# A causal convolution as diagonal matmuls, spaced pieces in the first scan, and fresh slot budgets

## The chip, the cores and the metric

The kernel runs on one core of a Trainium2 chip. A core has TensorE (PE in the profile; its weight loads are listed as PEld), VectorE (DVE), ScalarE (ACT), GpSimd (POOL), and the queue of SyncE (SP) that issues most DMAs. Each engine works through its own queue in order and waits for semaphores of the others. The metric is the device time of one launch in microseconds; of several runs the median counts.

## The reference, cut to what matters

The input is x of 4 batches, 256 positions and 256 features. A layer with a selective scan comes first, and then a layer with 16 attention heads and a mixture of 16 experts of which each token uses 4. All is float32.

```python
xz = einsum('bld,ed->ble', x, W_in); xp, z = split(xz, 2)          # 512 channels each
xpad = pad(xp, 3 positions ahead)
xc = silu(conv_b + sum(xpad[:, k:k + l, :] * conv_w[:, k] for k in range(4)))
dbc = einsum('ble,fe->blf', xc, W_x)                               # dt (128), Bm (16), Cm (16)
delta = softplus(einsum('blr,er->ble', dt, W_dt) + b_dt)
dA = exp(delta[..., None] * A); dBx = delta[..., None] * Bm * xc[..., None]
h = dA_t * h + dBx_t                                               # step by step, 16 states a channel
y = (einsum('bles,bls->ble', hs, Cm) + xc * Dp) * silu(z)
x = layernorm(x + einsum('ble,de->bld', y, W_out))
...
x = layernorm(x + ffn(x))                                          # attention, then the experts
```

The change bears on the sum over the four taps k for one of the four batches, and on the order of work around it.

## The kernel before

**Layout.** Channels lie on the 128 partitions. The 512 channels are four groups of 128, taken as two pairs p (0 and 1), so that a tile of 128x512 holds two groups of 256 positions. A *unit* is one of the 16 states n for one pair p, named n_p: 32 units make the scan of a batch, and 128 that of the four batches, in one stream.

**A unit.** decay (L463, ScalarE, two exponentials) writes da, of which there is one tile for each pair. feed (L472, GpSimd) writes dbx (three buffers). scan (L480, VectorE) writes h, a single buffer in PSUM. weigh (L487) multiplies by C into hc (two buffers), on VectorE, or for some units of the first batch (1_0, 2_1, 4_0 and so on) on GpSimd, where h lies in the hc tile itself. add is a pair of matmul pieces into y_ps for the first batch (L494, TensorE), and an addition on GpSimd (L492) for the others.

**The front of a batch.** conv_steps(b) projects a pair (project, L243, four matmuls, into one of the PSUM banks that bank() hands out in turn); last_tap (L259, ScalarE) multiplies by the last tap and adds the bias; tap (L251, VectorE) adds the other three taps for each of the two groups, six instructions a pair; tanh (L347, ScalarE) and one multiplication (L349, VectorE) make xc. delta_steps(b) projects xc to dbc (L362), copies B and C out (bc_sb, L367) and sends them through DRAM, from where they come back spread over all partitions (bc, L455, two loads for four units, two buffers), and begins delta (L377, L380, L383). soft_steps(b) ends the softplus: exp (L394), w (L398, L400), a logarithm (L407, with two loads of activation tables), additions on GpSimd and VectorE (L410, L413), and u = delta * xc (L415). z_steps(b) makes the gate.

**Two phases.** The first batch's front (first_front) is written out by hand. Then the first loop (N_RAMP = 34 units) runs the first batch's scan, and weaves in the front of the second batch, conv_steps(1), delta_steps(1), soft_steps(1). weave(engines) is called twice for each unit; in each call every row of jobs may give out its next piece, if that piece's engine is among those named; after a piece of TensorE, a piece of ScalarE or VectorE must let `lag` calls pass. Here lag is 2 and budgets do not hold pieces back (free=True), but their costs are taken off the budgets all the same.

Then come the slots (L1271), one for each of the 64 attention heads and three to end. A slot holds fixed pieces of three heads (projection of q and k at L591, scores, softmax, values, output at L672), three units of the scan in the first six slots and two after, and calls of weave, which hold a piece back while its engine's budget is below zero. At the start of each slot a budget gains a share (2816 for TensorE, 2000 for ScalarE and VectorE), up to that share. conv_steps(2), delta_steps(2), soft_steps(2) and z_steps(1) are jobs of the first 16 slots. After the last slot the remaining experts and the final norm follow.

SyncE's queue also carries 64 fills of a table in DRAM with zeros (L200), most of them during the first scan.

Of the kernel before, what the change touches and what calls it, by code (L numbers as in the profile page):

```python
# [10 lines left out]
F32 = mybir.dt.float32  # L11
I32 = mybir.dt.int32
AF = mybir.ActivationFunctionType
ALU = mybir.AluOpType
# [4 lines left out]
P = 128  # L19
B, S, D = 4, 256, 256  # L20
# [5 lines left out]
NC = DI // P  # L26
NS = 16
DC = 4
NH = 16
HG = 4  # L30
HD = 128
# [22 lines left out]
def block_kernel(  # L54
# [18 lines left out]
    nc = tc.nc  # L73
    TB = S // P
    NP = NC // 2
# [13 lines left out]

    chan_sb = const.tile([P, NC, DC + 3 + NS], F32, name="chan_sb")  # L90
    conv_w = lambda c, k: chan_sb[:, c, k : k + 1]
    conv_b = lambda c: chan_sb[:, c, DC : DC + 1]
    b_dt = lambda c: chan_sb[:, c, DC + 1 : DC + 2]
    d_skip = lambda c: chan_sb[:, c, DC + 2 : DC + 3]
    a_neg = const.tile([P, NC, NS], F32, name="a_neg")
    norms_sb = const.tile([P, 2, KD], F32, name="norms_sb")
    gate_sb = const.tile([P, KD, NE], F32, name="gate_sb")
    ident = const.tile([P, P], F32, name="ident")
# [10 lines left out]
    sh_down = const.tile([P, NSC, D], F32, name="sh_down")  # L109
    w_o_sb = const.tile([P, NH, D], F32, name="w_o_sb")  # L110

# [24 lines left out]
    m_w = mamba.enter_context(tc.tile_pool(name="m_w", bufs=1))  # L136
    m_x = mamba.enter_context(tc.tile_pool(name="m_x", bufs=2))
    m_keep = mamba.enter_context(tc.tile_pool(name="m_keep", bufs=1))
    m_two = mamba.enter_context(tc.tile_pool(name="m_two", bufs=2))
    m_tmp = mamba.enter_context(tc.tile_pool(name="m_tmp", bufs=4))  # L140
# [5 lines left out]
    w_x_sb = m_w.tile([P, NC, P + 2 * NS], F32, name="w_x_sb")  # L146
    w_dt_sb = m_w.tile([P, NC, P], F32, name="w_dt_sb")
    w_out_sb = m_w.tile([P, NC, D], F32, name="w_out_sb")

    xts = {}  # L150

# [17 lines left out]

    nc.vector.tensor_scalar_mul(chan_sb[:, :, 0 : DC + 1], chan_sb[:, :, 0 : DC + 1], 0.5)  # L170
    nc.scalar.activation(a_neg, chan_sb[:, :, DC + 3 :], AF.Exp)
    nc.vector.tensor_scalar_mul(a_neg, a_neg, -1.0)
# [35 lines left out]
    def bank(shape, name):  # L208
        banks.append(banks.pop(0))
        return banks[-1][0].tile(shape, F32, tag=banks[-1][1], name=name)  # L210
# [18 lines left out]
    OP, TINY = 60, 120  # L229
    PE, ACT, DVE, POOL, LATER = "PE", "ACT", "DVE", "POOL", "LATER"  # L230


    xcs, zss, deltas, us, ys, bcs = {}, {}, {}, {}, {}, {}

    def pair(pool, tag, b):
        return [pool.tile([P, 2, S], F32, tag=f"{tag}{p}", name=f"{tag}{b}_{p}") for p in range(NP)]

    def project(b, m, pt=None):
        if pt is None:
            pt = bank([P, 2, S], f"xz{b}_{m}")  # L240
        for j in range(2):
            for k in range(KD):
                nc.tensor.matmul(  # L243
                    pt[:, j, :], w_in_sb[:, m + j, k, :], xts[b][:, k, :], start=(k == 0), stop=(k == KD - 1)
                )
        return pt

    def tap(acc, pt, p, j):
        for k in range(DC - 1):
            o = DC - 1 - k  # L250
            nc.vector.scalar_tensor_tensor(  # L251
                acc[:, j, o:], pt[:, j, 0 : S - o], conv_w(2 * p + j, k), acc[:, j, o:], ALU.mult, ALU.add
            )

    def last_tap(b, p, pt):
        acc = m_tmp.tile([P, 2, S], F32, tag="t", name=f"acc{b}_{p}")
        for j in range(2):
            c = 2 * p + j
            nc.scalar.activation(acc[:, j, :], pt[:, j, :], AF.Identity, bias=conv_b(c), scale=conv_w(c, DC - 1))  # L259
        return acc  # L260

    def first_front():
# [70 lines left out]
        next_x(0)  # L333
        return y_ps

    def conv_steps(b):
        xc = xcs[b] = pair(m_two, "xc", b)
        for p in range(NP):
            yield PE, 4 * S
            pt = project(b, 2 * p)  # L340
            yield ACT, 2 * S
            acc = last_tap(b, p, pt)
            for j in range(2):
                yield DVE, 3 * (S + OP)
                tap(acc, pt, p, j)
            yield ACT, 2 * S
            nc.scalar.activation(pt, acc, AF.Tanh)  # L347
            yield DVE, 2 * S + OP
            nc.vector.scalar_tensor_tensor(xc[p], pt, 1.0, acc, ALU.add, ALU.mult)  # L349
# [201 lines left out]
    def load_v(b, g):  # L551
        wvs[b, g] = v_in.tile([P, KD * HG * HD], F32, tag="wv", name=f"wv{b}_{g}")
        nc.sync.dma_start(wvs[b, g], w_qkv[g][:, 2, :])

    class Values:
# [16 lines left out]
        def keep(self):  # L572
            b, g, i = self.b, self.g, self.i
            nc.scalar.copy(vs[b, g][:, i, :], self.pt)
            if i == TB - 1 and b * NH + (g + 1) * HG < B * NH:
                load_v(b + (g + 1) // (NH // HG), (g + 1) % (NH // HG))

# [79 lines left out]

    heads = [Head(b, hd) for b in range(B) for hd in range(NH)]


    def out_steps(b, slot):

        for hd in range(NH):
            while slot() < b * NH + hd + 3:
                yield LATER, 0
# [494 lines left out]

    budget = {PE: 0, ACT: 0, DVE: 0}

    def weave(*engines, lag=1, free=False):

        for name, row in work.items():
            while row:
                job = at_work.get(name) or next((j for j in row if j.may_begin(row)), None)
                if job is None:
                    break
                at_work[name] = job  # L1170
                if job.next is None or job.next[0] == LATER:
                    job.next = next(job.steps, ())
                if job.next:
                    engine, cost = job.next
                    job.since += 1
                    if engine not in engines or engine in (ACT, DVE) and job.since <= job.lag:
                        break
                    if not free and not job.urgent and budget.get(engine, 0) < 0:
                        break
                    if engine in budget:  # L1180
                        budget[engine] -= cost
                    job.next = next(job.steps, ())
                    job.lag, job.since = (lag if engine == PE else 0), 0
                if job.next:
                    if engine == DVE and job.next[0] == DVE:
                        continue
                    break
                row.remove(job)
                del at_work[name]

    def drain_all():
        for row in work.values():
            drain(*(job.steps for job in row))
            row.clear()
        at_work.clear()
# [23 lines left out]
        work["acc"].append(at(0, out_steps(b, slot_of)))  # L1219

    with tc.manual_schedule(engines=compute):
        y_ps = first_front()
        for u in units[0]:
            u.y_ps = y_ps
        stream[4].load()
        work["px"] += [Job(0, conv_steps(1)), Job(0, delta_steps(1))]
        work["soft"].append(Job(0, soft_steps(1)))
        for i, u in enumerate(stream[:N_RAMP]):
            if i == N_U - 2:
                drain_all()  # L1230
            if i == N_U:
                banks[:] = [(px_ps, "px"), (pq_ps, "pq")]
                end = end_steps(0, y_ps)
                next(end)
                next(end)
                sc_bank = sc_ps.tile([P, 512], F32, tag="sc", name="sc_bank")
                for _ in range(TB):
                    next(end)
            if i % 4 == 0 and i:
                stream[i + 4].load()  # L1240
            if i == 6:
                for r in results:
                    nc.sync.dma_start(
                        r.rearrange("(p i) d -> p i d", p=P), zeros[:, 0:D].unsqueeze(1).to_broadcast([P, NT, D])
                    )
                nc.sync.dma_start(w_o_sb, w_o)
                for c in range(NSC):
                    nc.sync.dma_start(sh_up[:, c], w_up[NRC + c])
                nc.sync.dma_start(sh_down, w_down[:, NRC:, :])
            n = stream[i + 2]  # L1250
            u.scan()
            n.feed()
            weave(PE, ACT, POOL, lag=2, free=True)
            u.weigh()
            n.decay()
            u.add()
            weave(PE, ACT, DVE, lag=2, free=True)

        turn = turn_steps(0)
        while 0 not in xns_of:  # L1260
# [6 lines left out]
        del stream[:N_RAMP]  # L1267
        load = iter(())
        values = None
        banks[:] = [(px_ps, "px")]  # L1270
        for now in range(B * NH + 3):  # L1271
            b, hd = divmod(now, NH)
# [59 lines left out]
            if h1:  # L1332
                h1.scores()
            weave(PE, ACT, DVE, POOL)
            if u0:
                u0.scan()
# [56 lines left out]
        b = B - 1  # L1393
# [3 lines left out]
        free = [(acc_ps, "acc")]  # L1397
# [94 lines left out]
```

## Time and profile before

| | us |
|---|---|
| median of 3 runs | 725.44 |
| lowest, highest | 723.23, 727.87 |
| the profiled execution | 721.92 |
| its span, first to last instruction | 720.2 |
| mean granted TensorE clock | 0.955 |
| POOL L472 (dbx), 128 instructions | 163.6 |
| DVE L480 (scan into h), 121 instructions | 148.3 |
| ACT L463 (da), 256 instructions | 122.2 |
| PE L591 (q and k), 512 pieces | 125.5 |
| DMA, mean rate over the span | 137 GB/s |

A float32 matmul shows as two pieces in the records. In the groups a line reads: line of the kernel, engine, operation, tile written <- tiles read, shape, number of instructions, then busy time. In the profile's 40 slices each slice is 18 us, a digit is the busy share in tenths, and PEclk is the share of full clock that TensorE was granted. In lines of waits, "A <- B: total, times, longest" says that A waited for B. In the list in order of time a line gives start, length, and in brackets the idle time before it and what ended it.

### The profile page before, as it was taken

How to read it: one execution, taken by the hardware profiler on the slowest of the kernel's cores; microseconds unless marked ns; L12 is line 12 of the kernel's file. 1: busy time of each engine (PE TensorE's matmuls, PEld its weight loads, DVE VectorE, ACT ScalarE, POOL GpSimd, SP SyncE). 2: the span in 40 equal slices, each digit the busy share in tenths (PEclk: the TensorE clock that was granted, in tenths of full speed). 3: DMA queues.
4: the chain of work that ended last, by engine and by line, in shares of the span. 5: the costliest groups of instructions: out<-in, count | busy, mean ns of one | idle time of the engine just before them, and what ended most of it. 6: DMA issues, size and time to landing. Idle time of an engine off the chain costs nothing. (4 is left out here: it accounts for less than half of the span.)

```text
span 720.2 us, 9834 instructions
## 1 busy us (share of the span) xinstructions
PE 637.2 (88%) x2760; PEld 470.3 (65%) x2760; DVE 469.5 (65%) x1164; ACT 429.7 (60%) x1128; POOL 435.0 (60%) x383
## 2 busy tenths in 40 slices
PE   8477575988989999699999999999999899999984
PEld 6233122665767767578877788877878577677753
DVE  4777888999677896968788876313323365666623
ACT  3645742776996879667698776465665431344421
POOL 2255985997898777898798797300400055366651
PEclk9779768999999999999999999999999999999997
DMA  8987878524433222234333432676840035456445
GB/s 301 326 283 243 261 238 275 157 76 119 101 98 109 87 91 88 75 92 135 105 114 102 120 121 61 184 200 168 258 128 16 0 55 137 88 89 101 59 56 162
DMA packets 91512, 98.62 MB, mean 137 GB/s; under 512 B 22720, under 2 KB 78016, under 8 KB 91328
## 3 DMA queue, kind: packets, MB, share of 16 engines
q1 hardware_dynamic: 82576, 87.42, 40.5%
q0 software_dynamic: 7296, 8.93, 7.0%
q10 hardware_dynamic: 1584, 1.62, 0.8%
q8 instruction: 24, 0.39, 0.2%
q14 instruction: 32, 0.26, 0.1%
HBM read 66.72 MB, written 32.26 MB: 137 GB/s over the span
## 5 line engine op out<-in xcount | busy, mean ns | idle before, releaser
L472 POOL TENSOR_TENSOR dbx<-u,bc 128x512 f32<-128x512 f32 x128 | 163.6, 1282 | 33.8 <-DMA bc<-bc_dram 19.1
L463 ACT ACTIVATE da<-de,a_neg 128x255 f32<-128x255 f32 x256 | 122.2, 478 | 55.3 <-DVE h L480 43.7
L480 DVE TENSOR_TENSOR_SCAN h<-da,dbx 128x512 f32<-128x512 f32 x121 | 148.3, 1225 | 8.3 <-POOL e L410 2.8
L492 POOL TENSOR_TENSOR y<-y,hc 128x512 f32<-128x512 f32 x96 | 122.2, 1274 | 34.9 <-DVE hc L487 19.1
L591 PE MATMUL pqk<-xnT,wqk 128*128 128x256 f32 x512 | 125.5, 389 | 1.5 <-issue 1.0
L591 PEld LDWEIGHTS pqk<-xnT,wqk 128*128 128x128 f32 x512 | 95.7, 196 | 14.3 <-PE tra L218 1.4
L1013 POOL DMA_INDIRECT results<-ys,b_to x40 | 62.0, 1551 | 54.8 <-ACT aT L1000 46.2
L487 DVE TENSOR_TENSOR hc<-h,bc 128x512 f32<-128x512 f32 x121 | 83.4, 689 | 12.2 <-PE y_ps L494 3.5
L609 DVE CUSTOM_DVE_ANT_0 pr<-sc_bank,mask 128x128 f32<-128x128 f32 (+1 forms) x128 | 40.5, 354 | 69.0 <-PE sc_bank L602 68.8
L672 PE MATMUL p_o<-w_o_sb,at 128*128 128x256 f32 x256 | 66.2, 381 | 6.7 <-ACT at L656 6.7
L564 PE MATMUL pv<-wv,xnT 128*128 128x512 f32 x128 | 63.1, 615 | 2.8 <-ACT qk L597 2.4
L494 PE MATMUL y_ps<-hc,ident 128*128 128x512 f32 x64 | 42.8, 788 | 24.1 <-POOL hc L487 12.8
L672 PEld LDWEIGHTS p_o<-w_o_sb,at 128*128 128x128 f32 x256 | 48.1, 190 | 16.6 <-ACT at L656 8.7
L597 ACT COPY qk<-pqk 128x512 f32<-128x512 f32 x64 | 37.3, 583 | 34.8 <-PE pqk L591 34.8
L623 ACT ACTIVATE pr<-pr,mx 128x128 f32<-128x128 f32 (+1 forms) x128 | 57.1, 451 | 0.9 <-DVE mx L609 0.9
L977 PE MATMUL gu<-w,xT 128*128 x160 | 54.1, 461 | 0.8 <-issue 0.8
L786 POOL DMA_INDIRECT rows<-xs,r_slot x32 | 32.6, 1018 | 32.9 <-DVE total L775 26.1
L646 ACT COPY pT<-pt 128x384 f32<-128x384 f32 x64 | 30.4, 476 | 36.4 <-PE pt L642 36.4
L637 ACT ACTIVATE pr<-pr,sm 128x128 f32<-128x128 f32 (+1 forms) x128 | 50.6, 443 | 1.6 <-DVE sm L633 1.6
L689 POOL TENSOR_SCALAR ss<-ss 128x2 f32<-128x2 f32 x4 | 0.8, 190 | 79.4 <-ACT xs L686 79.4
L494 PEld LDWEIGHTS y_ps<-hc,ident 128*128 128x128 f32 x64 | 13.7, 241 | 49.3 <-DVE hc L487 27.0
L1006 PE MATMUL yb<-w,aT 128*128 x160 | 41.5, 381 | 1.8 <-ACT aT L1000 1.8
(223 smaller groups left out, 1157.3 us busy)
## 6 DMA issues: line engine op xcount, KB each, us to landing
rows<-zeros SPq DMA_DIRECT2D x64, 288.0 KB, 5.3
bc<-bc_dram SPq DMA_DIRECT2D x66, 256.0 KB, 4.2
wqk<-in_w_qkv_dram SPq DMA_DIRECT2D x64, 256.0 KB, 2.9
wv<-in_w_qkv_dram SPq DMA_DIRECT2D x16, 512.0 KB, 3.7
xb<-rows SPq DMA_DIRECT2D x40, 144.0 KB, 2.2
results<-zeros SPq DMA_DIRECT2D x2, 1024.0 KB, 6.7
w_o_sb<-in_w_o_dram SPq DMA_DIRECT2D x1, 2048.0 KB, 10.7
w<-in_w_up_dram SPq DMA_DIRECT2D x8, 256.0 KB, 4.1
```

What stands on the lines that cost most here:

```text
L463: nc.scalar.activation(das[self.p][:, j, 1:], deltas[self.b][self.p][:, j, 1:], AF.Exp, scale=a_neg[:, 2 * self.p + j, self.n : self.n + 1],)
L472: nc.gpsimd.tensor_tensor(self.dbx, us[self.b][self.p], self.of_bc(0), ALU.mult)
L480: nc.vector.tensor_tensor_scan(flat(self.h), flat(das[self.p]), flat(self.dbx), 0.0, ALU.mult, ALU.add)
L487: (nc.gpsimd if self.on_pool else nc.vector).tensor_tensor(self.hc, self.h, self.of_bc(1), ALU.mult)
L492: nc.gpsimd.tensor_tensor(y, y, self.hc, ALU.add)
L494: nc.tensor.matmul(self.y_ps[self.p], ident, self.hc.rearrange("p b s -> p (b s)"), start=False, stop=(self.n == NS - 1),)
L564: nc.tensor.matmul(self.pt, xnTs[b][:, k, ts(i, P)], wvs[b, g][:, ts(k, HG * HD)], start=(k == 0), stop=(k == KD - 1),)
L591: nc.tensor.matmul(self.pq[:, j, :], self.w[:, j, k, :], xnTs[self.b][:, k, :], start=(k == 0), stop=(k == KD - 1))
L623: nc.scalar.activation(self.pr[:, cols], self.pr[:, cols], AF.Exp, bias=self.mx[:, j : j + 1], scale=-1.0, accum_out=self.sm[:, j : j + 1],)
L672: nc.tensor.matmul(pt[:, i, :], heads[b * NH + hd].at[:, ts(i, P)], w_o_sb[:, hd, :], start=False, stop=(i == TB - 1 and hd == NH - 1),)
L977: nc.tensor.matmul(gu, xT[:, k, :], w1[:, ds(x, 1), k::KD, :].rearrange("p x j f -> p (x j) f"), start=(k == 0), stop=(k == KD - 1),)
L1013: nc.gpsimd.indirect_dma_start(out=results[s % 2], out_offset=bass.IndirectOffsetOnAxis(to, axis=0), in_=ys, in_offset=None, bounds_check= ...
```

## The change

Three things. The second batch's taps become four 128x128 diagonal matrices for each group of channels, built once by GpSimd (turned_taps), and TensorE multiplies them with the projection, which ScalarE first copies to SBUF; the four products are added in PSUM, each shifted by its number of positions, and ScalarE adds the bias. The other batches keep the old convolution. In the first loop's weave a piece now waits one call after one of TensorE (before: two), and two calls wherever the engine changes otherwise (before: none), and pieces of GpSimd keep this distance too. Before the slots begin, the three budgets are set to 0. In the changed kernel's queues, SyncE's part also moves: the DMAs follow the pieces that issue or release them.

```diff
+BY_PE = (1,)
...
+    taps = m_w.tile([P, NC, DC, P], F32, name="taps")
...
+    def turned_taps():
+        for c in range(NC):
+            for k in range(DC):
+                nc.gpsimd.tensor_scalar(taps[:, c, k, :], ident, conv_w(c, k), None, ALU.mult)
+
+    def conv_by_pe(b):
+
+        xc = xcs[b] = pair(m_two, "xc", b)
+        for p in range(NP):
+            yield PE, 4 * S
+            pt = project(b, 2 * p)
+            yield ACT, 2 * S
+            xp = m_tmp.tile([P, 2, S], F32, tag="t", name=f"xp{b}_{p}")
+            nc.scalar.copy(xp, pt)
+            for j in range(2):
+                yield PE, 4 * S
+                if j == 0:
+                    pt = bank([P, 2, S], f"cv{b}_{p}")
+                for k in reversed(range(DC)):
+                    o = DC - 1 - k
+                    nc.tensor.matmul(
+                        pt[:, j, o:], taps[:, 2 * p + j, k, :], xp[:, j, 0 : S - o], start=(o == 0), stop=(k == 0)
+                    )
+            yield ACT, 2 * S
+            acc = m_tmp.tile([P, 2, S], F32, tag="t", name=f"acc{b}_{p}")
+            for j in range(2):
+                nc.scalar.activation(acc[:, j, :], pt[:, j, :], AF.Identity, bias=conv_b(2 * p + j))
+            nc.scalar.activation(pt, acc, AF.Tanh)
+            yield DVE, 2 * S + OP
+            nc.vector.scalar_tensor_tensor(xc[p], pt, 1.0, acc, ALU.add, ALU.mult)
+
     def conv_steps(b):
+        if b in BY_PE:
+            return conv_by_pe(b)
+        return conv_by_dve(b)
+
+    def conv_by_dve(b):
...
-    def weave(*engines, lag=1, free=False):
+    def weave(*engines, lag=1, free=False, other=0):
...
-                    if engine not in engines or engine in (ACT, DVE) and job.since <= job.lag:
+                    if engine not in engines or engine in (ACT, DVE, POOL) and job.since <= job.lag:
...
-                    job.lag, job.since = (lag if engine == PE else 0), 0
+                    job.lag, job.since = (lag if engine == PE else other if job.next and job.next[0] != engine else 0), 0
...
     with tc.manual_schedule(engines=compute):
+        turned_taps()
         y_ps = first_front()
...
-            weave(PE, ACT, POOL, lag=2, free=True)
+            weave(PE, ACT, POOL, lag=1, free=True, other=2)
...
-            weave(PE, ACT, DVE, lag=2, free=True)
+            weave(PE, ACT, DVE, lag=1, free=True, other=2)
...
+        budget.update({PE: 0, ACT: 0, DVE: 0})
```

## The prediction

> **What bounds the kernel now.** I read the page's first two sections, then the busy time by stage, then VectorE's waits in the first scan, then that stretch in order of time. On the page the reader is to see that TensorE is full only from the seventh slice on; before that its granted clock falls again and again, and VectorE carries the higher digits.
>
> ```profile
> PE 637.2 (88%) x2760; PEld 470.3 (65%) x2760; DVE 469.5 (65%) x1164; ACT 429.7 (60%) x1128; POOL 435.0 (60%) x383
> ...
> PE   8477575988989999699999999999999899999984
> PEld 6233122665767767578877788877878577677753
> DVE  4777888999677896968788876313323365666623
> ...
> PEclk9779768999999999999999999999999999999997
> ```
>
> By stage (columns: stretch; length, then busy time of PE, PEld, DVE, ACT, POOL; granted clock, DMA share, GB/s): the first scan (32 to 112.84), three stretches of slots (0 and 1, 2 to 5, 6 to 10, cut where the slots' L591 matmuls begin), and the slots after.
>
> ```profile
> 32.00:112.84 80.84, 56.92 (x106) 23.35 (x105) 66.36 (x77) 42.97 (x90) 58.66 (x47) 0.78 0.80 262
> ...
> 125.10:139.50 14.40, 12.88 (x43) 8.47 (x44) 13.31 (x19) 9.67 (x23) 12.53 (x11) 0.86 0.51 153
> 139.50:175.15 35.65, 29.83 (x129) 20.85 (x127) 33.72 (x65) 27.96 (x75) 33.23 (x28) 1.00 0.38 109
> 175.15:211.40 36.25, 33.45 (x148) 25.93 (x147) 25.34 (x51) 32.00 (x81) 29.86 (x24) 0.95 0.40 103
> 211.40:450.00 238.60, 228.70 (x1066) 180.20 (x1065) 188.82 (x413) 181.53 (x491) 198.20 (x171) 0.99 0.34 100
> ```
>
> VectorE bounds the first scan (66.36 of 80.84), TensorE what comes after 211 (96%). The queue order of the two kernels differs only up to slot 10, so whatever time is won or lost before 211 should arrive at the end unchanged. VectorE's waits in the first scan:
>
> ```profile
> DVE hc L487 <- PE y_ps L494: 3.5, 3, 1.6
> DVE bc_sb L367 <- PE dbc L362: 3.0, 1, 3.0
> DVE hc L480 <- PE y_ps L494: 3.0, 1, 3.0
> ```
>
> Its queue there, in order of time (start, length):
>
> ```profile
> 40.16 2.91 DVE L251 SCALAR_TENSOR_TENSOR acc<-xz,chan_sb,acc 128x253 f32<-128x253 f32 x6
> ...
> 51.62 0.69 DVE L487 TENSOR_TENSOR hc<-h,bc 128x512 f32<-128x512 f32 x1 [1.58 <-PE y_ps L494]
> 52.23 2.93 DVE L251 SCALAR_TENSOR_TENSOR acc<-xz,chan_sb,acc 128x253 f32<-128x253 f32 x6
> ...
> 63.72 0.41 DVE L367 COPY bc_sb<-dbc 32x256 f32<-32x256 f32 x1 [3.00 <-PE dbc L362]
> ...
> 67.11 1.21 DVE L480 TENSOR_TENSOR_SCAN h<-da,dbx 128x512 f32<-128x512 f32 x1
> ```
>
> Both groups of six taps stand in the scan's own queue, and so does the 3.00 us wait for the projection that follows.
>
> **Building the tap matrices.** Sixteen GpSimd multiplications of 128x128 are added after L194, which ends at 14.79. GpSimd has 128x128 copies at 0.28 us and one scaling (L183, 128x1024, 2.80 us, which with 0.19 us for a tiny one makes 0.52 for 128 columns). So 4.5 to 8.3 us, and GpSimd idles 15.65 us there until the bc load lands at 30.70: cost 0. Without that cover it would be the 4.5 to 8.3.
>
> **The first pair of the second batch's convolution.** Six taps (2.91) leave VectorE. Added: one ScalarE copy (a 128x512 copy, L597, 0.58) and 8 matmuls, which the records show as 16 pieces of 256 columns. The projection L243 has 8 such pieces in 1.89 us at full clock and 3.62 mostly at half, so 3.8 or 7.2. Walk along the new queues: the projection ends at 38.03, the copy at 38.65, the two L494 before the convolution at 39.75, so the convolution runs 39.8 to 43.6 (TensorE works without a break from 34.3, and at 37.87 four 128x512 pieces took 1.88, the full rate). Behind it in TensorE's queue stand the L494 of units 1_0 and 1_1; unit 2_0's L487 waits for the first, because hc has two buffers: 44.6 instead of 43.6. ScalarE adds the bias (1.02) and takes tanh (0.60) until 45.4, L349's successor ends at 46.05, and the decay of 2_1, queued behind that tanh, at 46.4. The scan of 2_1 starts at 46.45 and not at 47.70. Gain 1.25: 2.9 removed, some 1.65 of new waits.
>
> **The second pair.** The projection now follows 2_0's L494, so the 1.58 wait at 51.62 falls away. Convolution 50.2 to 54.0 at full clock, to 55.3 with one 3.4 us stretch at half. Behind it wait 3_1's L494, so 4_1's L487 (up to 1 us), then tanh, xc and the next decay: the scan of 5_0 starts between 56.9 and 58.1, before 64.06. L367 now stands behind one more scan, and waits 0.1 to 1 us for the 16 pieces of L362 (4.94 us before, half of it at half clock). The scan of 6_0 starts between 60.4 and 61.8 instead of 67.11: together with the first pair 5.3 to 6.7, I take 6.2. With both convolutions at half clock (7.2 each) the walk gives 3.4 less for the first and 2 less for the second, so some 1 us of gain is left; that is the lower end.
>
> The clock is the open point here. The row 73.80 to 77.20 has a clock of 0.63 although TensorE was busy 2.20 of 3.40 us, and its longest idle time there was 2.56 us. [...]
>
> **The spacing.** The ln block (two table loads of 1.28, two 128x512 of 0.62 in 1.15: 3.7 us of ScalarE) and the soft steps keep their lengths. L398 and L413, four VectorE operations between SBUF tiles beside a busy GpSimd, took 1.19, 0.57, 1.73 and 1.06 here, against 0.42 and 0.69 while GpSimd was idle (23.07 and 27.42). They only move, from 77 to 91 to some 75 to 105; I keep their price. What the spacing can save is their queueing (0.85 us before 10_0's scan, 1.34 at 77.11, both not sure to go); the ln block, now between the decays of units 12_0 and 12_1, must cost up to 0.6. Net 0, between -2.0 and +1.0. In the last ten units GpSimd works 1.27 of each 2.15 us, and the 8.8 us left hide the six soft steps (7.6), some of which come earlier; uncovered they would cost what is over. On SP's queue, the store of bc_sb goes behind the load of bc_8; its reader comes 30 us later. The fills issue at 0.84 us (seven in 5.88), and at most seven stand between two bc loads, 6.7 us with the load, against 7.0 to 8.6 us for four units: hidden, narrowly.
>
> **The fresh budgets.** They move batch 2's convolution (by VectorE, as before) and its delta and soft steps from slots 2 to 10 to slots 0 to 7. Nothing is added; what counts is the busiest engine of each stretch. Slots 0 and 1: VectorE 13.31 + 5.84 taps + 1.37 xc = 20.5. Slots 2 to 5: ScalarE 27.96 - 3.2 (bias and tanh) + 11.0 (dt 0.4, abs and relu 3.3, exp 1.2, y 1.8, z 0.6, ln block 3.7) = 35.8; GpSimd 34.5. Slots 6 to 10: GpSimd 29.86 - 1.27 = 28.6, TensorE 33.45 - 5.8 = 27.7. Sum 84.9 us, 1.4 less than the 86.3 of now. But stretches are never full: now they last 5.8 longer than their busiest engines, which would give 90.7 (+4.4), and a walk through slots 0 and 1, where the first pqk waits behind a projection and the taps behind its bias, ends at 149 instead of 139.5+6, which gives +6.8. The 2.35 us wait for a bc load at 179.75 and the 1.1 of the first stretch are likeliest to recur: 84.9 + 3.4 = 88.3, so +2.0, between -1.4 and +6.8.
>
> **Sum.** -6.2 + 0 + 2.0 = -4.2. The profiled execution took 721.92 us (span 720.2, 1.7 around it), so 717.7. It lies below the median of the three runs, 725.44; from that, 721.2.
>
> **Rivals.** (a) The taps' 5.84 and the 3.0 wait go, the slots pack better because 6 to 10 lose what filled them: ramp -7 to -8, slots -1.4 to -3. For it: slots 6 to 10 show ScalarE, TensorE and GpSimd all above 29.8 of 36.25. Against: the first stretch has VectorE at 92% already. Some -10: 715.5. (b) The clock stays at half through both convolutions: ramp -1, slots +2, so 726.4. For it: 0.78 mean clock. Against: the added work itself fills TensorE. (c) Slower: the early start of batch 2 piles taps on VectorE in slots 0 and 1 and 11 us on ScalarE in slots 2 to 5, so that GpSimd, continuously busy from 127 to 166 now, runs dry. At +6.8 with the ramp's 6.2 it is +0.6; it decides from 6.2 on, and if slots 2 to 5 also lose the 3.7 us ln block whole, it is +4.3: 729.7. (d) The budgets do nothing because other work gates the jobs: ruled out by the queue order, where batch 2's first projection stands before the first pqk; without it -6.2, 719.2.
>
> **Chances.** About 1% (7.25 us) is what a measurement can tell from no change. Forecast 0.48 (721.2), (a) 0.27, (b) 0.13, (c) 0.12. Faster by over 1% (below 718.2): (a) and a little of the forecast, 0.30. Slower by over 1% (above 732.7): the end of (c), 0.06. Within 1%: 0.64. Range: from (a)'s middle less its own spread, 714, to (c)'s point less 1.7, 728; the three runs alone spread over 4.6.
>
> **What would show it.** Right: no L251 between 32 and 110; the scan stage near 74.6 us; VectorE's wait for dbc under 1 us; slots 0 and 1 near 20 us, slots 6 to 10 near 31; the rest after slot 11 as long as before. Wrong: a VectorE wait for y_ps of over 2 us beside each convolution (b); slots 0 to 10 above 92 us (c) or below 85 (a); or the stretch after slot 11 longer than now, which no step here foresees.

## The result, and the profile after

| | before | after |
|---|---|---|
| median of four runs, us | 724.77 | 712.91 |
| lowest, highest | 723.23, 727.87 | 710.35, 713.79 |
| profiled execution (span) | 721.92 (720.2) | 712.83 (710.5) |
| granted clock in it | 0.955 | 0.968 |

The ratio is 0.9837, interval 0.9803 to 0.9871: 11.9 us by the medians, 9.1 by the two profiled executions. The forecast was 721.2, between 714 and 728. The direction was right and the size was not: the median lies 1.1 us under the range. Of the 2.8 us between the two measures nearly all is the distance of the first profiled execution from its own median.

The page after, with the same rows as before:

```profile
PE 636.4 (90%) x2792; PEld 472.1 (66%) x2792; DVE 463.7 (65%) x1152; ACT 430.3 (61%) x1130; POOL 443.9 (62%) x399
...
PE   8498576788999999799999999999999799999984
PEld 6264124466677767678777878878787577777753
DVE  3777888987878878967888965322313375666623
...
PEclk9799978999999999899999999999999999999998
```

VectorE did 5.8 us less; TensorE stands at 9 from the eleventh slice on, before from the thirteenth (the 17th, the 32nd and the last two slices excepted in both); and the clock's third and fifth digits are 9 where they were 7. By stage, as in the prediction (length; busy PE, PEld, DVE, ACT, POOL; clock, DMA share, GB/s), with slots cut where their q and k matmuls (now L630) begin:

```profile
32.00:104.52 72.52, 56.98 (x138) 25.98 (x138) 60.63 (x65) 43.57 (x93) 57.69 (x48) 0.87 0.93 274
119.50:140.80 21.30, 17.01 (x61) 10.14 (x60) 19.37 (x37) 13.57 (x33) 15.48 (x14) 0.92 0.58 150
140.80:173.70 32.90, 28.25 (x128) 21.43 (x127) 24.45 (x42) 30.01 (x74) 31.47 (x26) 1.00 0.37 105
173.70:202.70 29.00, 27.27 (x125) 20.35 (x124) 26.14 (x55) 25.72 (x71) 29.00 (x24) 1.00 0.47 120
202.70:441.30 238.60, 229.10 (x1070) 180.84 (x1069) 188.73 (x413) 181.92 (x492) 197.36 (x170) 0.99 0.35 100
```

The first scan takes 72.5 us and not 80.8. Between it and the first q and k matmul lie 15.0 us, 2.7 more (a projection of the third batch now stands ahead). Slots 0 and 1 take 6.9 more, slots 2 to 5 take 2.75 less, slots 6 to 10 take 7.25 less, slot 11 some 0.9 less. From slot 12 on every slot begins 9.6 us earlier than before (9.2 to 9.8), and the span is 9.7 shorter; the last row, as long as the prediction's, holds as much TensorE work as that (229.10 and 228.70). VectorE's waits in the first scan:

```profile
DVE hc L519 <- ACT da L502: 3.3, 2, 3.0
DVE hc L526 <- PE y_ps L533: 2.3, 3, 1.4
...
DVE bc_sb L406 <- PE dbc L401: 0.9, 1, 0.9
```

and its queue, in order of time:

```profile
45.04 0.69 DVE L368 SCALAR_TENSOR_TENSOR xc<-cv,acc 128x512 f32<-128x512 f32 x1
46.00 1.22 DVE L519 TENSOR_TENSOR_SCAN hc<-da,dbx 128x512 f32<-128x512 f32 x1 [0.27 <-ACT da L502]
...
54.94 0.69 DVE L526 TENSOR_TENSOR hc<-h,bc 128x512 f32<-128x512 f32 x1 [1.38 <-PE y_ps L533]
55.58 0.69 DVE L368 SCALAR_TENSOR_TENSOR xc<-cv,acc 128x512 f32<-128x512 f32 x1
56.54 1.23 DVE L519 TENSOR_TENSOR_SCAN h<-da,dbx 128x512 f32<-128x512 f32 x1 [0.27 <-ACT da L502]
...
60.61 0.41 DVE L406 COPY bc_sb<-dbc 32x256 f32<-32x256 f32 x1 [0.92 <-PE dbc L401]
60.95 1.21 DVE L519 TENSOR_TENSOR_SCAN h<-da,dbx 128x512 f32<-128x512 f32 x1
```

The two groups of six taps are gone. The scan behind the first convolution starts at 46.00 (47.70 before), the one behind the projection at 60.95 (67.11 before). On TensorE:

```profile
39.90 3.60 PE L359 MATMUL cv<-xp,taps 128*128 128x256 f32 x16
...
50.44 3.60 PE L359 MATMUL cv<-xp,taps 128*128 128x256 f32 x16
...
56.74 3.84 PE L401 MATMUL dbc<-xc,w_x_sb 128*32 128x256 f32 x16
```

Both convolutions took 3.60 us, and the projection, which took 4.94 before, 3.84: all three at the full clock (granted 1.00 from 39.90 to 60.60).

### The profile page after: what moved, and what is told of

It is laid out like the page before. It is cut to its first block, busy times and chain, and to the rows that moved or that the text cites. A ratio compares the mean times of both kernels' runs of the same rounds, so it can differ in the third digit from the quotient of the medians.

```text
span 710.5 us, 9912 instructions
## 1 busy us (share of the span) xinstructions
PE 636.4 (90%) x2792; PEld 472.1 (66%) x2792; DVE 463.7 (65%) x1152; ACT 430.3 (61%) x1130; POOL 443.9 (62%) x399
## 5 line engine op out<-in xcount | busy, mean ns | idle before, releaser
L511 POOL TENSOR_TENSOR dbx<-u,bc 128x512 f32<-128x512 f32 x128 | 163.0, 1279 | 13.7 <-DMA bc<-bc_dram 11.6
L519 DVE TENSOR_TENSOR_SCAN h<-da,dbx 128x512 f32<-128x512 f32 x121 | 148.3, 1226 | 11.9 <-ACT da L502 6.6
L630 PE MATMUL pqk<-xnT,wqk 128*128 128x256 f32 x512 | 122.0, 381 | 1.6 <-ACT v L613 1.6
L630 PEld LDWEIGHTS pqk<-xnT,wqk 128*128 128x128 f32 x512 | 93.6, 192 | 12.9 <-ACT v L613 2.2
L533 PE MATMUL y_ps<-hc,ident 128*128 128x512 f32 x64 | 38.5, 711 | 15.7 <-DVE hc L526 9.6
L690 PE MATMUL av<-pT,v 128*128 128x256 f32 x128 | 39.0, 386 | 1.7 <-ACT pT L685 1.7
```

Of the source, the lines that this page charges most:

```text
L511: nc.gpsimd.tensor_tensor(self.dbx, us[self.b][self.p], self.of_bc(0), ALU.mult)
L519: nc.vector.tensor_tensor_scan(flat(self.h), flat(das[self.p]), flat(self.dbx), 0.0, ALU.mult, ALU.add)
L630: nc.tensor.matmul(self.pq[:, j, :], self.w[:, j, k, :], xnTs[self.b][:, k, :], start=(k == 0), stop=(k == KD - 1))
```

## The experiments

Theory: the three parts each have a price of their own, the matmuls by relieving VectorE, the distances (the calls that a piece must let pass, the spacing of the prediction) by the waits they take out of the first scan, the budgets by moving pieces between slots. Rivals: it is TensorE's clock that gains; the budgets alone gain in slots 6 to 10; the parts only gain together. The marks used: when bc_sb is copied out (the projection), when the first result leaves the first scan (L511 before, L550 after), the time from there to the start of slot 12, and from slot 12 to 24. The kernels of one group were timed on the same chip against the kernel before; a chip changes the absolute time (the kernel before had medians of 723.57, 732.18 and 735.51 on three), so ratios are compared, and marks up to slot 24.

| kernel | bc_sb | first result | to slot 12 | 12 to 24 | ratio, interval |
|---|---|---|---|---|---|
| before | 63.72 | 112.84 | 109.20 | 95.08 | 1 |
| before_again | 63.01 | 112.47 | 110.63 | 96.37 | 0.9989, 0.9952 to 1.0025 |
| budgets_alone | 64.70 | 113.95 | 109.76 | 95.08 | 0.9980, 0.9941 to 1.0019 |
| spacing_alone | 71.95 | 112.17 | 112.15 | 97.66 | 1.0053, 1.0022 to 1.0083 |
| no_taps (spacing, budgets) | 72.05 | 112.26 | 108.30 | 95.09 | 0.9975, 0.9944 to 1.0007 |
| taps_alone | 59.58 | 106.86 | 109.54 | 95.62 | 0.9910, 0.9872 to 0.9949 |
| no_spacing (taps, budgets) | 60.93 | 108.04 | 110.63 | 95.09 | 0.9920, 0.9890 to 0.9950 |
| taps_and_spacing | 61.10 | 104.37 | 110.19 | 96.44 | 0.9910, 0.9876 to 0.9944 |
| after | 60.61 | 104.52 | 107.94 | 95.08 | 0.9837, 0.9803 to 0.9871 |
| changed_again | 60.15 | 103.56 | 108.50 | 95.10 | 0.9833, 0.9787 to 0.9879 |

**One part, two parts.** In the kernels with old budgets, the budgets at the first slot are set to what the kernel before has there (the ramp of the changed kernel would leave others):

```
taps_and_spacing, against the changed kernel:
-        budget.update({PE: 0, ACT: 0, DVE: 0})
+        budget.update({PE: -5120, ACT: -8960, DVE: -7224})
taps_alone: this, and
-                    if engine not in engines or engine in (ACT, DVE, POOL) and job.since <= job.lag:
+                    if engine not in engines or engine in (ACT, DVE) and job.since <= job.lag:
-            weave(PE, ACT, POOL, lag=1, free=True, other=2)
+            weave(PE, ACT, POOL, lag=2, free=True)
-            weave(PE, ACT, DVE, lag=1, free=True, other=2)
+            weave(PE, ACT, DVE, lag=2, free=True)
budgets_alone, against the kernel before:
+        budget.update({PE: 0, ACT: 0, DVE: 0})
spacing_alone, against the kernel before: the three lines of the distances
```

> Only the diagonal matmuls: the old spacing of the first loop, and the budgets set to what they were before (PE -5120, ACT -8960, DVE -7224), so that the slots have the order of the kernel before. Theory (the parts add as the stages of the profile after show: 6.2 us up to the scan of unit 6_0, 2.2 later in the first scan, 1.3 in the slots): the first scan ends about 106.5 instead of 112.84, the slots last as before, and the time is 6 to 6.5 us less, ratio about 0.991. Rival one (the convolution gives all, the rest does nothing): 9 to 11 us less, 0.986. Rival two (the old spacing spoils it, because a half of the convolution stands on either side of an L494): 3 to 4 us less, 0.995.

> The changed kernel with the budgets of before (PE -5120, ACT -8960, DVE -7224) at the start of the slots; slots in the order of before. Theory: the first scan ends at 104.5 as in the changed kernel, the slots 0 to 10 last 86.3 as before, the time is 8.3 us less, ratio 0.9885, and the changed kernel is 1.3 us below it. The forecast's step (fresh budgets cost 2): 10 us less or more, 0.986, the changed kernel above it.

> The kernel before with the budgets set to 0 ahead of the slots; the taps tile stands unused. Theory: first scan unchanged to 112.84; slots 0 and 1 some 9.5 us longer, 2 to 5 some 3 shorter, 6 to 11 some 8 shorter, in sum 1.3 less, ratio 0.998. The forecast's step: 2 us more, 1.003. A rival that explains why the medians differ by more than the two profiles (11.9 against 9.1): fresh budgets are worth 4 us, 0.9945.

> The kernel before with the new spacing in the first loop alone (taps on VectorE, budgets not set afresh). Theory (spacing helps whatever stands in the queue): first scan ends 2.2 us earlier, 0.997. Rival (it only helps behind the diagonal matmuls, because soft steps come later by the shortened queue): within 0.5 us of before, 0.9995.

taps_alone: 717.43 us, first result 6.0 earlier than in the kernel before, and 5.1 of it are left at the end of the span. taps_and_spacing: 717.57, and 6.0 at the end, where 8.3 was expected. Its first result comes 2.5 earlier than that of taps_alone, though the projection is no earlier. VectorE's waits from the projection on, in taps_alone and then in taps_and_spacing:

```profile
DVE hc L519 <- ACT da L502: 2.7, 1, 2.7
DVE hc L526 <- PE y_ps L533: 1.9, 2, 1.3
DVE bc_sb L406 <- PE dbc L401: 0.2, 1, 0.2
```

```profile
DVE bc_sb L406 <- PE dbc L401: 0.9, 1, 0.9
DVE h L519 <- ACT da L502: 0.8, 1, 0.8
```

4.8 us of waits become 1.7. The long one is a piece of the batch's front that stands too early in ScalarE's queue. ScalarE in taps_alone, in order of time:

```profile
65.66 1.91 ACT L502 ACTIVATE da<-de,a_neg 128x255 f32<-128x255 f32 x4
70.70 0.84 ACT L419 ACTIVATE e<-p_de,chan_sb 128x256 f32<-128x256 f32 x2 [3.14 <-PE p_de L416]
71.43 0.99 ACT L502 ACTIVATE da<-de,a_neg 128x255 f32<-128x255 f32 x2
```

L419 waits 3.14 us for its matmul, and the decay that the next scan needs is queued behind it. The matmul itself stood behind two pieces of y_ps that waited 2.67 us for a product of GpSimd, and GpSimd had waited 2.22 us for a bc load. With the distances L419 comes later, and there it waited for nothing:

```profile
67.19 0.83 ACT L419 ACTIVATE e<-p_de,chan_sb 128x256 f32<-128x256 f32 x2
...
68.63 1.00 ACT L502 ACTIVATE da<-de,a_neg 128x255 f32<-128x255 f32 x2
```

(This is the changed kernel; its queues in the first scan are those of taps_and_spacing.)

spacing_alone was slower than the kernel before, which neither expectation had. The distances push the second pair's taps 3.1 us back (52.23 to 55.36), its xc 6.6, and the copy behind the projection 8.2. TensorE runs dry between its y_ps pieces:

```profile
40.08 1.12 PE L533 MATMUL y_ps<-hc,ident 128*128 128x512 f32 x2 [1.91 <-POOL hc L526]
43.49 4.22 PE L533 MATMUL y_ps<-hc,ident 128*128 128x512 f32 x4 [2.29 <-DVE hc L526]
...
60.25 4.24 PE L533 MATMUL y_ps<-hc,ident 128*128 128x512 f32 x4 [2.28 <-DVE hc L526]
...
67.09 4.83 PE L401 MATMUL dbc<-xc,w_x_sb 128*32 128x256 f32 x16
```

Four pieces of y_ps took 1.88 us in the changed kernel at 60.41 and 4.2 here. From the projection to the first result spacing_alone is faster than the kernel before (40.22 against 49.12), which gives back the 8.2 and 0.7 more, but the slots after it were 5.5 longer up to slot 24 than in the first profile of the kernel before (2.8 longer than in the second). The order of the queues doesn't explain that: idle_matmuls (below), whose slots have the order of the kernel before, was 5.4 longer there too. idle_matmuls shows a granted clock of 0.92 in this stretch against 0.96, and 5.1 us more on TensorE (184.6 against 179.5). All ten timed executions of spacing_alone had 0.941 to 0.943 over the span, the 31 of the kernel before on that chip 0.946 to 0.961. What brought the lower clock is not shown.

budgets_alone shows the rearrangement by itself: slot 2 began 12.5 later than in the kernel before and slot 12 only 1.7 later, so that slots 2 to 11 gave back 10.8, as in the changed kernel (from 1.2 later to 9.6 earlier). The work is moved, and TensorE's share of it did not change: in the stretch from the first result to slot 12 TensorE was busy 92.3 us of 109.2 in the kernel before and 91.6 of 107.9 in the changed one.

**The changed kernel again, without the distances, and with more matmuls.**

```
no_spacing: the three lines of the distances as in taps_alone, the budgets begin afresh
pe12, pe123, against the changed kernel:
-BY_PE = (1,)
+BY_PE = (1, 2)
+BY_PE = (1, 2, 3)
```

> The changed kernel once more, on the same chip as the next three. Theory (the profiled executions give the size of the change, 721.92 to 712.83, a ratio of 0.987): 0.985 to 0.989 against the kernel before. Rival (the medians give it, 0.9837): 0.982 to 0.985. The end of the first scan near 104.5 us of the span and slot 12 some 9.6 us earlier than in the kernel before, in either.

> The diagonal matmuls and the fresh budgets, with the distances of the kernel before in the first scan. Theory: the spacing is worth what it was at the end of the first scan with the diagonal matmuls, some 2.5 us, and the budgets rearrange slots 0 to 11 whatever the ramp ended with: last result of the first scan near 107 us, slots from 12 on some 7 us before those of the kernel before, a time 2 to 3 us above that of the changed kernel. Rival: the fresh budgets absorb it, since TensorE is the bound of slots 6 to 11 and only waits less there: time within 1 us of the changed kernel's.

> The changed kernel with the third batch's convolution on TensorE as well as the second's. Theory: slots 0 and 1 last longer in the changed kernel because VectorE's multiply-adds of the third batch's convolution lie there, ahead of the chunks that its softplus and scans need; without them slots 0 and 1 take 5 to 6 us less, and the end comes 3 to 6 us before that of the changed kernel. Rival: those slots wait for TensorE or ScalarE, which the new matmuls (4 groups of 16, 3.60 us each while the clock is full) only load further: the end comes 0 to 7 us later than the changed kernel's.

> Second, third and fourth batch's convolution on TensorE. Theory: the fourth batch's front lies in slots that TensorE binds (from slot 12 on the slots follow its matmuls in both kernels), so its 64 matmuls add their own time there, some 7 to 14 us above the run with two batches. Rival: VectorE binds those slots too, and the time is that of the run with two batches or 2 to 4 us less.

changed_again gave 720.18 on a chip where the kernel before had 732.18: 0.9833, so the medians' 12 us stand, and slot 12 began 10.0 earlier than in the first profile of the kernel before. Its span, 719.3, is longer than the first one's 710.5 only behind slot 55 (2.9 us from there to slot 63, 6.2 after it). All eight kernels that were profiled on the later two chips show such a loss there, of 6.1 to 11.3 us together, so it is not of the change.

no_spacing took 725.24, 5.1 us over changed_again, where the theory had 2 to 3 and the rival 1. 4.5 of it was there at the first result (108.04 against 103.56), and the same wait stood in ScalarE's queue, 2.96 us for p_de.

pe12 went against its theory. Taking the third batch's taps off VectorE made the time from the first result to slot 2 shorter by 2.1 us, and slots 2 to 11 longer by 8.1. In busy time, pe12 from the first result to slot 2 and on to slot 12:

```profile
102.38:137.04 34.66, 27.01 (x105) 19.95 (x106) 26.49 (x45) 16.02 (x39) 24.62 (x22) 0.90 0.67 207
137.04:216.82 79.78, 72.77 (x309) 54.22 (x309) 58.27 (x106) 64.69 (x167) 69.47 (x57) 0.96 0.37 100
```

changed_again, the same stretches:

```profile
103.56:140.34 36.78, 26.84 (x89) 17.08 (x90) 31.53 (x56) 16.74 (x40) 23.67 (x22) 0.84 0.66 202
140.34:212.06 71.72, 66.48 (x293) 50.76 (x293) 56.76 (x107) 62.91 (x164) 70.28 (x57) 0.98 0.37 109
```

Both stretches together are 5.9 us longer, with 6.5 us more on TensorE and 3.5 less on VectorE. The median is 726.03, 5.9 above. The new matmuls themselves lie ahead of slot 2 or end with its begin (118.0 to 137.2), and behind that TensorE is not full (72.77 of 79.78). GpSimd is the busiest engine of slots 2 to 11 in changed_again, 70.28 of 71.72 us; in pe12 it waits 9.1 us there for products of VectorE (1.4 in changed_again). The longest of these waits begins with the third batch's xc, which stands in VectorE's queue ahead of a scan and waits for its tanh on ScalarE. VectorE's line, then GpSimd's:

```profile
140.99 0.69 DVE L368 SCALAR_TENSOR_TENSOR xc<-cv,acc 128x512 f32<-128x512 f32 x1 [4.50 <-ACT cv L366]
```

```profile
143.70 1.27 POOL L531 TENSOR_TENSOR y<-y,hc 128x512 f32<-128x512 f32 x1 [4.11 <-DVE hc L526]
```

So the rival had the sign; a TensorE that binds slots 2 to 11 is not what the trace shows. pe123, 731.90, pays again: 5.9 us over pe12, just outside the 7 to 14 expected, and with the sign of the theory. Its stretch from slot 24 to 55 takes 204.11 us against 196.73 in changed_again, with TensorE busy for 199.72 and 194.94 of them; the new matmuls lie ahead of it (244 to 265) and push other work there. Both expectations counted the matmuls double: a batch adds 32 pieces, 7.2 us at 0.225 us each, and not 64.

**The clock, the length of the matmuls, and the rest.**

```
idle_matmuls, against the kernel before, in conv_steps(1):
+            if b == 1:
+                spare = bank([P, 2, S], f"spare{p}")
+                for k in range(16):
+                    nc.tensor.matmul(
+                        spare[:, k // 8, :], ident, w_in_sb[:, 0].rearrange("p k q -> p (k q)"), start=(k % 8 == 0), stop=(k % 8 == 7)
+                    )
one_tap, against the changed kernel:
-                for k in reversed(range(DC)):
...
+                nc.tensor.matmul(pt[:, j, :], taps[:, 2 * p + j, DC - 1, :], xp[:, j, :], start=True, stop=True)
no_taps, against the changed kernel:
-BY_PE = (1,)
+BY_PE = ()
-        turned_taps()
before_again: the kernel before
```

> The kernel before with 32 matmuls more and nothing else: where the second batch's two pairs are projected, 16 matmuls with 128x256 moving (3.60 us at the full clock) go into a bank that nothing reads; the queues of the other engines are the same. Theory (part of what the diagonal matrices gain is that TensorE stays busy there and so keeps the full clock): no half clock between about 43 and 60, dbc in 3.84 us in place of 5.48, the projection copied out 1.5 to 3 us earlier than at 63.72, and a time 0 to 3 us under the kernel before. Rival (the gain is VectorE's relief alone): the clock falls as before or the matmuls only stand ahead of y_ps in TensorE's queue, and the projection comes 0 to 4 us later, with a time 0 to 4 us above the kernel before.

> The changed kernel without three of the four taps of the second batch's convolution: 4 diagonal matmuls a pair in place of 16, so 2.7 us less on TensorE a pair; VectorE, ScalarE and GpSimd have the same queues. Theory (the diagonal matmuls' length is on the path from the projection to the next scan only in part, and keeps the clock full): the half clock comes back between 45 and 60, dbc takes 5 us or more in place of 3.84, and the projection is copied out within 1.5 us of the changed kernel's 60.61. Rival (only the work counts): the projection comes 4 to 5.4 us earlier, at 55 to 57, and the end 3 to 5 us earlier.

> The distances and the fresh budgets with the convolution of the kernel before. Theory: without the diagonal matmuls the distances cost at the second batch's projection what they gain behind it (as in the run with the distances alone), and the fresh budgets move the slots without a net gain: last result of the first scan at 112 to 113, time within 3 us of the kernel before, 1.000 to 1.006. Rival (distances and fresh budgets gain together, whatever the convolution): 5 us less than the kernel before, 0.990 to 0.995.

> The kernel before once more, for a second profiled execution. Theory (the first profiled execution lay among the shorter of its executions, and what separates the longer ones is more stretches at half the clock): an execution of 725 us or more shows a mean granted clock of 0.946 to 0.950 against 0.955, and its loss lies in the first scan and the slots up to 24. Rival (the longer executions lose in the transfers or elsewhere): the clock is as before and the loss lies elsewhere.

idle_matmuls asked whether a busy TensorE is the gain. Its expectation had the price wrong: a float32 matmul shows as two pieces, so 16 of them took 7.07 us and not 3.60.

```profile
39.35 7.07 PE L346 MATMUL spare<-w_in_sb,ident 128*128 128x256 f32 x32
...
61.01 3.84 PE L368 MATMUL dbc<-xc,w_x_sb 128*32 128x256 f32 x16
```

The clock did stay full from 37 to 77 us (granted 1.00), and the projection took 3.84 instead of 4.94. But the y_ps pieces stand behind the idle matmuls, and the projection was copied out at 64.89, 1.2 later than before. Ratio 0.9989, 0.9949 to 1.0029. So a full clock with VectorE's taps left in won nothing, at this length; what a shorter filling would give was not tried.

one_tap, without three quarters of the matmuls, lay between its two expectations: bc_sb at 58.69, 1.9 earlier, though 5.1 us had been taken off TensorE. So 3.2 of the 5.1 us were beside other work. The half clock didn't come back (1.00 in every stretch of 3 to 6 us from 40 to 70), against the theory. Its ratio, 0.9819 with 0.9759 to 0.9878, doesn't tell it from the changed kernel.

no_taps confirms spacing_alone in the first scan: projection copied out at 72.05, first result at 112.26. Its ratio is just under the expected range, and 0.8% under that of spacing_alone: beside the new distances the budgets gained.

before_again missed: that execution had the lower clock (0.950) but lost 6.0 us between slots 55 and 63 and 5.2 behind, as the other kernels on that chip did, and only 2.4 up to slot 24. So it doesn't show what separates the executions of one kernel on the first chip.

No kernel here that computes the whole of it was faster than the changed one.

## Why the prediction was wrong in size

**Tap matrices at no cost: right, though longer.** The sixteen multiplications took some 9.5 us (14.49 to 24.21, with another piece between) and not 4.5 to 8.3, and GpSimd still idled 6.78 us behind them until the bc load. The first scan began at 32.28 (32.00 before).

**First and second pair, -6.2: right.** The walk's times were 46.45 and 60.4 to 61.8, the trace has 46.00 and 60.95. As a part by itself, first results at 106.86 and 108.04 (mean 107.45) stand against 112.84, 112.47 and 113.95 (mean 113.09), all with the old distances: -5.6. Rival (b), half clock in the convolutions, fell: 3.60 us each, at a granted clock of 1.00. The scan of 6_0 came 6.16 us earlier.

**The spacing, "Net 0, between -2.0 and +1.0": wrong, with the matmuls -3.3.** First results at 104.52, 104.37 and 103.56 (mean 104.15) against 107.45. The prediction named queueing of 0.85 and 1.34 us as all that could be saved, from the waits of the kernel before. It didn't ask which waits would appear once the projection came 6 us earlier with the old distances: L419's 3.14 for its matmul, with a decay behind it. Without the matmuls the same edit gained 0.9 at that mark (mean of 112.17 and 112.26).

**The fresh budgets, "+2.0, between -1.4 and +6.8": wrong.** The stretch from the first result to slot 12 was 109.20, 110.63, 109.54, 110.19 and 112.15 in the five executions with old budgets, and 107.94, 108.50, 109.76, 110.63 and 108.30 in the five with fresh ones: means of 110.34 and 109.03, -1.3, with an overlap. (idle_matmuls, old, had 112.01; one_tap, fresh, 108.96.) Its two halves don't overlap. Slots 2 to 11 took 71.7 us in each of the five with fresh budgets and 82.5 to 83.1 with old ones. What lies ahead of slot 2 took 26.7 to 29.1 with old budgets, 36.3 to 36.8 with fresh budgets and new distances, and 38.1 and 38.9 with fresh budgets and old distances. So the budgets gain beside the new distances, and nothing beside the old ones. The ratios say the same: 0.9910 to 0.9837 and 1.0053 to 0.9975 with new distances (the intervals lie just apart in both pairs), 1 to 0.9980 and 0.9910 to 0.9920 with old ones. That speaks for the rival by which parts only gain together, as far as these two go, and no step of the prediction had it.

From slot 12 to 24, where the queues don't differ, the means of the five are 96.23 and 95.09, -1.1: these fresh ones are all within 0.02 us (one_tap had 95.93), the old ones scatter. That this 1.1 comes from the budgets is not shown, since the time lost to half clock there also differs between kernels with the same budgets (3.42 us in before, 6.82 in idle_matmuls, see the end).

In the two profiled executions alone the prediction's three stretches went from 86.3 to 83.2 (under the 85 that the prediction gave as a sign of rival (a)), 2.7 came ahead of them and slot 11 lost 0.9: -1.3. Slots 0 and 1 were forecast right (near 20, 21.3 came). Slots 2 to 5 took 32.9 where ScalarE's 35.8 was said to bound them; it was busy 30.01 there. The 11.0 us of batch 2 all came, but the rest did not stay as the sum kept it: 21 exponentials of decays in place of 26 (2.4 us less), 6 exponentials of the softmax with their sums in place of 10 (2.4 less) and 3 copies of pT in place of 5 (1.0 less) fell into this stretch. Slots 6 to 10 took 29.0, within 0.4 of the 28.6 forecast for the busiest engine, GpSimd, and not "near 31". The 3.4 us of waits carried over from the old slots did not recur: in slots 2 to 11 GpSimd was busy 70.24 of 71.67 us (73.69 of 82.50 before). Rival (c) fell with it: GpSimd did not run dry, it was busy 31.47 of 32.90 us in slots 2 to 5.

**The base.** -5.6 - 3.3 - 1.3 = -10.2, and -11.3 with the 1.1 of slots 12 to 24, near the -11.9 of the medians. The prediction's sum was made against an execution 2.85 under its kernel's median; and its 12-to-24 stretch, 95.08, is the shortest of the old ones. Of 31 executions of the kernel before on one chip, 21 had spans of 719.1 to 721.9, at clocks of 0.955 to 0.961, and ten 724.2 to 728.0, eight of these at 0.946 to 0.950. The profiled one belonged to the shorter ones.

**The rivals.** (a), "slots pack better", with 715.5, was nearest; its mechanism (slots 6 to 10 lose what filled them) is seen, at -7.25, but slots 0 and 1 take most of it back, and much of the gain came from the spacing, for which there was no rival. So its number was near in part by luck. The rest after slot 11 was as long as before, as foreseen.

**Two readings.** TensorE was not "full only from the seventh slice on": the page before has it at 9 throughout from the thirteenth. And the row 73.80 to 77.20 doesn't show half clock beside partly busy work: most of its 2.56 us of idleness lies ahead of it (72.4 to 75.0), and the half clock began at 74.66 (0.50 from there to 77.20), as the last section shows.

What stays open: why the budgets gain only beside the new distances, beyond the 2 us ahead of slot 2, and how much of it is the clock. The mean clock of the timed executions goes with it in part (0.963 to 0.968 in the changed kernel, 0.957 to 0.963 in changed_again, 0.954 to 0.962 in taps_and_spacing), on different chips. Two executions of one kernel can have the half clock at other places: a stretch of it begins at 43.94 in before and at 43.1 in before_again. How much of the scatter of equal queues this makes was not tested.

## What to carry to other kernels

When an edit takes a wait out of a queue, walk on from the new time: in-order queues hold pieces placed for the old one, and the next piece that stands too early takes part of the gain, or gives it when another edit moves it. Offloading to TensorE gained where it idled between the pieces of a scan that VectorE bound (5.6 us). For the third batch it cost 5.9 us, with the result waiting in VectorE's queue ahead of a scan that GpSimd needed, and for the fourth 5.9 more, in slots where TensorE was busy 98% of the time. Two changes of order can gain together what neither gains alone; a sum of single prices misses that. Compare a sum with the median and with the spread of the marks, not with one execution's.

## What the runs showed of the hardware

- Half clock came in stretches of 3.41 us or multiples of it. In before, between 40 and 140 us, the granted clock was 0.50 from 43.94 to 50.77, 57.59 to 61.01, 74.66 to 78.07, 81.49 to 84.90, 88.31 to 95.14, 101.97 to 108.79 and 122.45 to 129.27, and 1.00 elsewhere; in after, 0.50 from 74.99 to 78.41, 92.06 to 102.30, 112.54 to 119.36 and 133.02 to 136.43. Within each of these two profiles the starts are whole multiples of 3.41 us apart. In before_again, the same kernel as before, a stretch begins at 43.1 and not at 43.94 (granted 0.53 from 43.00 to 45.00).
- From slot 12 to 24, where the queues don't differ, the time lost to half clock, added over windows of 2 us, was 3.40 to 3.42 us in before, before_again, after and no_taps (6.8 us at half), 5.10 in one_tap (10.2) and 6.82 in idle_matmuls (13.6).
- Half clock also followed partly busy work. Two times 3.41 us of the kernel before, each with the 3.41 us behind it:

```profile
40.53:43.94 3.41, 1.13 (x2) 0.30 (x2) 3.27 (x7) 1.31 (x3) 2.29 (x2) 1.00 0.80 271
43.94:47.35 3.41, 2.29 (x3) 1.18 (x4) 3.22 (x5) 1.49 (x4) 1.80 (x2) 0.50 0.32 98
...
71.25:74.66 3.41, 1.19 (x3) 0.30 (x2) 3.17 (x5) 3.27 (x9) 2.20 (x2) 1.00 0.98 299
74.66:78.07 3.41, 3.07 (x4) 1.38 (x5) 1.97 (x3) 3.09 (x8) 3.41 (x4) 0.50 0.69 203
```

  TensorE (first of the busy times) was busy 1.13 and 1.19 us at a clock of 1.00, and the 3.41 us behind ran at 0.50. Ahead of the seven stretches of before listed above it was busy 1.13, 0.44, 1.19, 1.28, 1.22, 1.57 and 0.00 of 3.41 us, ahead of the four of after 1.36, 1.27, 0.29 and 1.50. What sets the clock is not shown by this.
- Gaps of 1.90 and 2.29 us on TensorE, with 1.13 us of work between them, stood ahead of the half clock from 43.94 on in before. one_tap's gaps between 40 and 70, up to 1.34 us, stood beside a granted clock of 1.00 in every window there.
- Chips differ: medians of the kernel before of 723.57, 732.18 and 735.51 on three. In the profiles of the later two the difference lies mostly behind slot 55 (against before 11.2 us in before_again, 10.3 in idle_matmuls, 9.2 in one_tap and 8.0 in no_taps).
